# Pool totals the softmax's sums over the partitions, in place of TensorE's products with ones

## The chip, the core and the metric

The kernel runs on one core of a Trainium2 chip. A core has TensorE (matrix products, PE in the profile), VectorE (DVE), ScalarE (ACT) and GpSimd (POOL, called Pool here), each with its own queue that is worked off in order, and SyncE (SP), whose queue issues the DMAs. The metric is the device time of one execution in microseconds (us); a run's value is the median of its executions.

## The reference

A block of attention and then a small step behind it, for 4 batches of 1024 tokens with 1024 channels, all in 32-bit floats. `x` is normalized, scaled and shifted by a condition, projected to queries, keys and values of 16 heads, and each head's softmax weighs its values; the result is projected and added:

```python
xn = _rms_norm(x, g_norm) * (1.0 + scale) + shift
qkv = xn @ W_qkv                        # 16 heads of 64
q, k = _rms_norm(q, g_q), _rms_norm(k, g_k)
logits = einsum('bhqd,bhkd->bhqk', q, k) * d ** (-0.5)
attn = softmax(logits, axis=-1)
o = einsum('bhqk,bhkd->bhqd', attn, v)
x = x + o + o @ W_out
x = x + (causal convolution of x over 4 tokens, channel by channel) + b
```

## The kernel before, in words

**Units.** Two heads form a pair; a pair's 1024 queries are worked in two halves of 512. One pair and one half is a `Unit`: 4 batches x 8 pairs x 2 halves = 64 units. Keys lie on the partitions, 128 at a time (8 steps, `kt`), queries of both heads along the rows (2 x 512). For one unit:

- `scores(kts)`: TensorE writes 128 keys x 2 x 512 queries into a PSUM tile of tag "s" (two such buffers); ScalarE copies it to an `sp` tile (line 696); from the second tile on, `running` (line 705, VectorE) keeps the running maximum `mx`.
- `softmax()` calls nothing at once but puts steps on a list, each with a due time: `maximum` (line 710, one all-reduce over partitions with max on Pool), `broadcast` (line 719, ScalarE copies the result into a PSUM tile of tag "s"), and for each of the 8 tiles `shift` (line 724, VectorE subtracts) and `weigh` (line 728 on ScalarE takes the exponential; line 730 on Pool adds the tile to `sum`).
- `values(kts)`: TensorE multiplies the weights by the values into `pav` (line 751).
- `finish()`: TensorE totals `sum` over the partitions by four products with a 128 x 32 tile of ones (line 766), one for each quarter of the 1024 queries, into a PSUM tile of tag "m".
- `spread` (line 784 and on): ScalarE copies the totals to SBUF; four DMAs write 256 totals each to DRAM (line 787), and one DMA reads them back as `few`, 128 partitions x 8 (line 789).
- `invert`: VectorE takes the reciprocal of `few` (line 792), a DMA writes it to DRAM (line 794), and two DMAs read it back, repeated over 64 partitions for each head, as `rec` (line 797).
- `divide`: VectorE multiplies `pav` by `rec` (line 806), and a DMA stores the result for the output product (line 810).

The last two units (batch 3, last pair) total all 512 columns in each product and invert the totals directly on VectorE (line 804), without the DMAs.

**The order.** TensorE's, VectorE's, ScalarE's and Pool's instructions run in the order in which the program emits them. A clock in the program, `clock[0]`, decides that order: `tick(us)` moves it on by an assumed duration and then runs all deferred steps that are due, in the order of their due times; `defer(delay, key, step)` puts a step on the list, due `delay` after the clock; `need(key)` runs the steps of that key at once. A score of one tile and the values of one tile tick 0.9 each (`PAIR`), a piece of the QKV product 2.65 (`TIME`), four transposes 0.45.

The main loop goes through the 64 units. Work of other kinds (pieces of the QKV product of pairs to come, transposes, output products, stores) is cut into four stretches. For unit p, with `last` the unit before it:

```python
unit.scores((0, 1)); need("exp", last.name); last.values(range(0, HT))
fill(); unit.scores((2, 3)); fill(); last.values(range(4, 6))
unit.scores((4, 5)); last.values(range(6, NT)); last.finish()
fill(); unit.scores((6, 7)); need("mx", unit.name); unit.softmax()
defer(DIVIDE, ..., last.divide); fill()
```

The fourth `fill` is the long one (26 on the clock, 22 in batch 0); the first three are mostly empty. The due times of the softmax are counted from `softmax()`: the maximum at 2.6, the broadcast at 6.5, the subtraction of tile kt at 7.6 + kt x 1.8 (1.6 in batch 0), the exponential and the addition 1.3 after it.

**Buffers.** The tag "xs" has two buffers of 128 x 512 for squares of `x` (`Norm.squares`), for a few rows at the start and for the modulation; the tag "xg" has two of 128 x 1024, for chunks of `x` that are transposed (`Chunk.load`). `sum` and the maximum share one buffer (tag "sum").

Of the kernel before, what the change touches and what calls it, by code (L numbers as in the profile page):

```python
# [10 lines left out]
F32 = mybir.dt.float32  # L11
# [4 lines left out]
P = 128  # L16
# [5 lines left out]
def kernel(  # L22
# [32 lines left out]
    nc = tc.nc  # L55
    B, N, DIM = x.shape
    D = DIM // HEADS
    NJ = DIM // P
    NT = N // P
    HN = N // 2  # L60
# [7 lines left out]
    QN = N // 4  # L68
# [6 lines left out]
    apool = ctx.enter_context(tc.tile_pool(name="apool", bufs=1))  # L75
    small = ctx.enter_context(tc.tile_pool(name="small", bufs=2))
    ps_s = ctx.enter_context(tc.tile_pool(name="ps_s", bufs=2, space=bass.MemoryType.PSUM))
    ps_m = ctx.enter_context(tc.tile_pool(name="ps_m", bufs=3, space=bass.MemoryType.PSUM))
    dram = ctx.enter_context(tc.tile_pool(name="dram", bufs=1, space=bass.MemoryType.DRAM))
# [16 lines left out]
    def defer(delay, key, step):  # L96
        pending.append((clock[0] + delay, next(serial), key, step))
# [10 lines left out]
    def tick(us):  # L108

        clock[0] += us  # L110
        flush(lambda e: e[0] <= clock[0])
# [11 lines left out]
    def fill_gap(us):  # L123
        for e in sorted(idle, key=lambda e: e[2][2][0] != "qk"):
            if e[2] not in pending:
                idle.remove(e)
            elif e[0] <= clock[0] and e[1] <= us:
                us -= e[1]
                idle.remove(e)
                pending.remove(e[2])  # L130
                e[2][3]()
# [8 lines left out]
    def need(*key):  # L140
        flush(lambda e: e[2] == key)
# [26 lines left out]
    R_COND, R_G, R_CB, R_BE = 0, TAPS * NJ, (TAPS + 1) * NJ, (TAPS + 2) * NJ  # L168
    R_GQ = R_BE + 2 * NJ
    NR = R_GQ + 2  # L170
    rows = apool.tile([P, HN], F32, tag="xs", name="rows", bufs=2)[:NR, :P]
    nc.sync.dma_start(rows[R_COND:R_G, :], cond.rearrange("k (j p) -> (k j) p", p=P))
    nc.sync.dma_start(rows[R_G:R_CB, :], g_norm.rearrange("(j p) -> j p", p=P))
    nc.sync.dma_start(rows[R_CB:R_BE, :], conv_b.rearrange("(j p) -> j p", p=P))
# [36 lines left out]
    class Norm:  # L211


        def __init__(self, b, tiles):
            self.b, self.tiles = b, tiles
            n = len(tiles)
            self.name = f"{b}_{tiles[0]}"
            self.ss = small.tile([P, NT * 2], F32, tag="ss", name=f"ss_{self.name}", bufs=1)
            self.ss = self.ss[:, : n * 2].rearrange("p (i g) -> p i g", i=n)
            self.rn = small.tile([P, NT], F32, tag="rn", name=f"rn_{self.name}")[:, :n]  # L220

        def squares(self, i):
            t0 = self.tiles[i] * P
            for g in range(2):
                xs = apool.tile([P, HN], F32, tag="xs", name=f"xs_{self.name}_{i}_{g}", bufs=2)
                nc.sync.dma_start(xs, x[self.b, t0 : t0 + P, g * HN : (g + 1) * HN])
                defer(5.0 + g, ("x", self.name), lambda xs=xs, g=g: self.square(xs, xs, i, g))

# [2 lines left out]

        def squares_of(self, i, halves):
            for g in range(2):
                to = apool.tile([P, HN], F32, tag="xs", name=f"xs_{self.name}_{i}_{g}", bufs=2)
                self.square(halves[g], to, i, g)

        def root(self):
# [143 lines left out]
    class Embed:  # L381
# [22 lines left out]
        def run(self):  # L404
            half = self.half
            ps = ps_m.tile([P, 512], F32, tag="m", name=f"mod_ps_{half}")[:, :QN]
            for k in range(NJ):
                for g in range(4):
                    nc.tensor.matmul(
                        ps[32 * g : 32 * (g + 1), :],  # L410
                        condT[:, k, :],
                        self.w[k][g // 2][:, g % 2 * QN : (g % 2 + 1) * QN],
                        start=(k == 0),
                        stop=(k == NJ - 1),
                    )
            sb = apool.tile([P, HN], F32, tag="xs", name=f"mod_sb_{half}", bufs=2)[:, :QN]
            nc.scalar.copy(sb, ps)

            mt = ps_m.tile([P, 512], F32, tag="m", name=f"modT_ps_{half}")[:, :QN]
            mt = mt.rearrange("p (i g b) -> p i g b", i=2, g=4)  # L420
            for i in range(2):
                nc.tensor.transpose(mt[:, i].rearrange("p g b -> p (g b)"), sb[:, i * P : (i + 1) * P], ident)
            for s in range(2):
                c = s * NJ + half * KH
                nc.vector.tensor_add(
                    mod[:, c : c + KH, :].rearrange("p (u i) b -> p u i b", u=2),
                    mt[:, :, 2 * s : 2 * s + 2, :B].rearrange("p i u b -> p u i b"),
                    cols[:, R_BE + c : R_BE + c + KH]
                    .rearrange("p (u i) -> p u i", u=2)
                    .unsqueeze(3)  # L430
                    .to_broadcast([P, 2, 2, B]),
                )
            js = slice(half * KH, (half + 1) * KH)
            nc.vector.scalar_tensor_tensor(
                gain[:, js, :],
                mod[:, js, :],
                1.0,
                cols[:, R_G + half * KH : R_G + (half + 1) * KH].unsqueeze(2).to_broadcast([P, KH, B]),
                ALU.add,
                ALU.mult,  # L440
            )
# [235 lines left out]
    class Unit:  # L677
        def __init__(self, pr, half):
            self.pr, self.half = pr, half
            self.name = f"{pr.b}_{pr.c}_{half}"  # L680
            self.sp = []

# [43 lines left out]
        def weigh(self, kt):  # L726
            sp = self.sp[kt]
            nc.scalar.activation(sp, sp, AF.Exp)  # L728
            if kt:
                nc.gpsimd.tensor_tensor(self.sum, self.sum if kt > 1 else self.sp[0], sp, ALU.add)  # L730

        def softmax(self):

            key = ("exp", self.name)
            loud[0] = clock[0] + TO_SHIFT + TO_EXP
            step = STEP if self.pr.b else STEP_FIRST
            loud[1] = loud[0] + NT * step + LOUD
            defer(TO_MAX, key, self.maximum)
            defer(TO_MAX + 0.1, key, lambda: fill_gap(GAP))
            defer(TO_SPREAD, key, self.broadcast)  # L740
            for kt in range(NT):
                at = TO_SHIFT + kt * step
                defer(at, key, lambda kt=kt: self.shift(kt))
                defer(at + TO_EXP, key, lambda kt=kt: self.weigh(kt))

        def values(self, kts):
            if kts[0] == 0:
# [10 lines left out]
                tick(PAIR)  # L758

        def finish(self):  # L760
            b, c = self.pr.b, self.pr.c
            tot = ps_m.tile([P, HN], F32, tag="m", name=f"tot_{self.name}")
            for g in range(4):
                h, i = divmod(g, 2)
                some = slice(0, HN) if (b, c) == (B - 1, NJ - 1) else slice(i * QN, (i + 1) * QN)
                nc.tensor.matmul(  # L766
                    tot[32 * g : 32 * (g + 1), : some.stop - some.start],
                    ones,
                    self.sum[:, h, some],
                    start=True,  # L770
                    stop=True,
                )
            tick(2 * PAIR)
            self.tot = tot
            if (b, c) == (B - 1, NJ - 1):
                return
            key = ("tot", self.name)
            defer(0.2, key, lambda: self.spread(tot))
            defer(8.0, key, self.invert)

        def spread(self, tot):

            sums = apool.tile([P, HN], F32, tag="rec", name=f"tots_{self.name}", bufs=1)
            nc.scalar.copy(sums[:, :QN], tot[:, :QN])
            scr = dram.tile([4, QN], F32, tag=f"tot_{self.name}", name=f"scrT_{self.name}")
            for g in range(4):
                nc.sync.dma_start(scr[g : g + 1, :], sums[32 * g : 32 * g + 1, :QN])
            self.few = small.tile([P, 2 * HN // P], F32, tag="few", name=f"few_{self.name}", bufs=1)
            nc.sync.dma_start(self.few, scr.rearrange("g (p i) -> (g p) i", p=32))

        def invert(self):
            nc.vector.reciprocal(self.few, self.few)
# [6 lines left out]
        def divide(self):  # L799
            b, c = self.pr.b, self.pr.c  # L800
            need("tot", self.name)
            if (b, c) == (B - 1, NJ - 1):
                self.rec = apool.tile([P, HN], F32, tag="rec", name=f"rec_{self.name}", bufs=1)
                nc.vector.reciprocal(self.rec, self.tot)
            oT = apool.tile([P, HN], F32, tag="oT", name=f"oT_{self.name}", bufs=2)
            nc.vector.tensor_mul(oT, self.pav, self.rec)
            if (b, c) == (B - 1, NJ - 1):
                oTs[b, c, self.half] = oT
                return
            nc.sync.dma_start(scrO[b][self.half][:, c, :], oT)  # L810
# [260 lines left out]
    TO_MAX, TO_SPREAD, TO_SHIFT, TO_EXP, STEP = 2.6, 6.5, 7.6, 1.3, 1.8  # L1071
# [241 lines left out]
    for T in range(NPR):  # L1313
        for step in START.get(T, ()):
            step()
        run(piece(T))
# [6 lines left out]
    for p in range(B * NB):  # L1323
# [10 lines left out]
        def fill():  # L1334
            run(next(stretches))
# [68 lines left out]
```

## Time and profile before

| | |
|---|---|
| time, median of 3 runs | 2848.15 us (2846.98 to 2849.5) |
| span of the profiled execution, first to last instruction | 2846.5 us |
| TensorE busy / its share | 2764.2 us / 97% |
| VectorE | 2161.3 us / 76% |
| ScalarE | 1541.5 us / 54% |
| Pool | 1345.1 us / 47% |
| DMA | 509.40 MB, mean 179 GB/s |
| granted TensorE clock, mean | 0.995 |

The span leaves out what lies ahead of the first and behind the last instruction: 1.65 us by the median. A line of the profile that gives a group of instructions reads: line, engine, operation, output <- inputs, shape, count | busy us, mean ns of one | idle time of the engine just ahead of them, and what ended it. A line of a timeline reads: start us, duration us, engine, line, operation, and in brackets the idle time ahead of it and what ended it. PEld is TensorE's loading of weights, SPq the queue of SP; "x8" behind a product with four calls counts two passes of each.

### The profile page before, as it was taken

Reading aid. Unit: us, or ns where it says so; the run is one execution under the profiler, and the core shown is the slowest. Engines: PE = TensorE matmul, PEld = TensorE weight load, DVE = VectorE, ACT = ScalarE, POOL = GpSimd, SP = SyncE. Lnnn points to the kernel's source line nnn. Section 1 sums busy time; section 2 is a strip of 40 time slices with the busy share of each in tenths; the row PEclk is TensorE's granted clock in tenths of the full one; section 3 lists DMA queues with packets and bytes.
Section 4 is the critical chain, followed back from the end, with each engine's and each line's share of the span. In section 5 each row is a group of like instructions: output and inputs, shape, how many; then the busy total and the mean of one; then the engine's idle time right before and its main releaser. Section 6 shows DMA issues by size and latency. Waiting matters only on the chain.

```text
span 2846.5 us, 31973 instructions
## 1 busy us (share of the span) xinstructions
PE 2764.2 (97%) x10581; PEld 1310.7 (46%) x10581; DVE 2161.3 (76%) x2579; ACT 1541.5 (54%) x2221; POOL 1345.1 (47%) x534
## 2 busy tenths in 40 slices
PE   6999999999999999999999999999999999999998
PEld 3544444444444444444444445445444444443344
DVE  4688887888888777777877777787877877687863
ACT  4255656655555556655555556665555545555532
POOL 2056554565654453553555355355445445554520
PEclk9999999999999999999999999999999999999999
DMA  9844555644565566665565556666556444533334
GB/s 318 280 168 145 193 174 184 211 152 169 174 196 159 174 196 205 214 229 164 162 207 186 165 178 212 203 218 198 163 202 211 141 130 159 167 109 96 118 108 118
DMA packets 416844, 509.40 MB, mean 179 GB/s; under 512 B 40816, under 2 KB 326824, under 8 KB 406952
## 3 DMA queue, kind: packets, MB, share of 16 engines
q1 hardware_dynamic: 416680, 507.36, 55.1%
q8 instruction: 85, 1.39, 0.2%
q14 instruction: 79, 0.65, 0.1%
HBM read 411.85 MB, written 95.40 MB: 178 GB/s over the span
## 4 chain that ended last, share of the span: by engine, by line
PE 78%; DVE 11%; DMA 4%; ACT 3%; issue 2%; POOL 2%; SPq 1%; DVEq 0%; ACTq 0%; POOLq 0%
PE pqkv_P L648 29%; PE pav L751 15%; PE s L688 15%; PE po L1009 5%; PE po_P L940 4%; PE po L940 4%; DVE sp L724 3%; DVE mx L705 3%; POOL sum L730 1%; PE qkt L506 1%; PE tot L766 1%; DMA scrR<-few 1%; DVE qk L498 1%; PE po L995 1%; ACT sp L696 1%
## 5 line engine op out<-in xcount | busy, mean ns | idle before, releaser
L648 PE MATMUL pqkv_P<-w_P,a 128*128 128x384 f32 x3456 | 1172.5, 490 | 15.5 <-issue 5.6
L730 POOL TENSOR_TENSOR sum<-sum,sp 128x1024 f32<-128x1024 f32 x384 | 956.8, 2492 | 36.5 <-ACT sp L728 5.7
L648 PEld LDWEIGHTS pqkv_P<-w_P,a 128*128 128x128 f32 x3456 | 639.4, 190 | 478.7 <-issue 69.2
L696 ACT COPY sp<-s 128x1024 f32<-128x1024 f32 x512 | 506.0, 1015 | 507.4 <-PE s L688 459.1
L705 DVE TENSOR_TENSOR mx<-mx,sp 128x1024 f32<-128x1024 f32 x384 | 518.9, 1351 | 170.9 <-ACT sp L696 143.8
L728 ACT ACTIVATE sp<-sp 128x1024 f32<-128x1024 f32 x512 | 531.8, 1055 | 204.6 <-DVE sp L724 201.3
L724 DVE TENSOR_TENSOR sp<-sp,mbp 128x1024 f32<-128x1024 f32 x512 | 604.2, 1210 | 19.3 <-ACT mbp L719 19.3
L710 POOL PARTITION_ALL_REDUCE mb<-mx x64 | 219.2, 3426 | 826.5 <-DVE mx L705 785.0
L688 PE MATMUL s<-qT,kT 64*128 64x512 f32 x2048 | 516.3, 620 | 21.8 <-DVE sp L724 17.0
L751 PE MATMUL pav<-sp,v 128*64 128x512 f32 x2048 | 486.5, 607 | 0.0
L730 POOL TENSOR_TENSOR sum<-sp,sp 128x1024 f32<-128x1024 f32 x64 | 151.5, 2367 | 485.6 <-ACT sp L728 232.9
L688 PEld LDWEIGHTS s<-qT,kT 64*128 64x128 f32 x2048 | 174.9, 186 | 314.8 <-issue 200.0
L751 PEld LDWEIGHTS pav<-sp,v 128*64 128x64 f32 x2048 | 131.2, 137 | 331.9 <-issue 322.2
L1045 DVE SCALAR_TENSOR_TENSOR y<-x,cols,y 128x512 f32<-128x512 f32 x192 | 224.3, 1173 | 47.9 <-ACT y L1033 43.3
L705 DVE TENSOR_TENSOR mx<-sp,sp 128x1024 f32<-128x1024 f32 x64 | 113.2, 1769 | 102.1 <-ACT sp L696 102.0
L667 DVE TENSOR_TENSOR qk<-u,pqkv_P 128x256 f32<-128x256 f32 x256 | 106.2, 415 | 77.9 <-PE pqkv_P L648 76.5
L1009 PE MATMUL po<-ob,wo 128*128 128x512 f32 x352 | 155.3, 593 | 0.0
L940 PE MATMUL po_P<-o_P,wq_P 128*128 128x512 f32 x320 | 143.9, 592 | 0.0
L498 DVE TENSOR_TENSOR qk<-qk,ms 128x1024 f32<-128x1024 f32 x64 | 129.7, 2047 | 0.0
L719 ACT COPY mbp<-mb 128x1024 f32<-128x1024 f32 x64 | 65.2, 1018 | 111.0 <-POOL mb L710 111.0
L940 PE MATMUL po<-o_P,wq_P 128*128 128x512 f32 x240 | 108.0, 592 | 0.0
L485 ACT ACTIVATE sq<-qk 128x512 f32<-128x512 f32 x128 | 76.7, 627 | 53.6 <-DVE qk L667 53.6
(94 smaller groups left out, 1730.7 us busy)
## 6 DMA issues: line engine op xcount, KB each, us to landing
a<-scrA SPq DMA_DIRECT2D x212, 512.0 KB
w_P<-scrB SPq DMA_DIRECT2D x64, 768.0 KB
o_P<-scrS SPq DMA_DIRECT2D x40, 1024.0 KB
w_P<-in_L_cond_W_qkv_dram SPq DMA_DIRECT2D x192, 192.0 KB
o_P<-scrO SPq DMA_DIRECT2D x30, 1024.0 KB
scrA<-r SPq DMA_DIRECT2D x28, 896.0 KB
wq_P<-scrW SPq DMA_DIRECT2D x70, 256.0 KB
xc<-in_x_dram SPq DMA_DIRECT2D x64, 256.0 KB
```

What stands on the lines that cost most here:

```text
L648: nc.tensor.matmul(pm, (chunk.r(place) if a is None else a[:, k, :])[:, t % 2 * P : (t % 2 + 1) * P], w[:, k, :], start=(k == 0), stop=(k ...
L688: nc.tensor.matmul(ps[:, h, :], pr.kT[kt // HT][h * D : (h + 1) * D, kt % HT * P : (kt % HT + 1) * P], pr.qT[self.half][h * D : (h + 1) * ...
L696: nc.scalar.copy(sp, ps)
L705: nc.vector.tensor_max(self.mx, self.mx if kt > 1 else self.sp[0], self.sp[kt])
L710: nc.gpsimd.partition_all_reduce(self.mb.rearrange("p h q -> p (h q)"), self.mx.rearrange("p h q -> p (h q)"), P, bass_isa.ReduceOp.max,)
L724: nc.vector.tensor_sub(self.sp[kt], self.sp[kt], self.mb)
L728: nc.scalar.activation(sp, sp, AF.Exp)
L730: nc.gpsimd.tensor_tensor(self.sum, self.sum if kt > 1 else self.sp[0], sp, ALU.add)
L751: nc.tensor.matmul(self.pav[h * D : (h + 1) * D, :], self.pr.v[kt // HT][:, kt % HT, h * D : (h + 1) * D], self.sp[kt][:, h, :], start=(kt ...
L940: nc.tensor.matmul(pm, self.w[name][:, k, :], self.o[name][:, k, :], start=(k == 0 and name not in ("P2", "P3", "P4")), stop=(k == KH - 1),)
L1009: nc.tensor.matmul(self.pm, self.w[kh][:, k % KH, :], oTs[b, k, half], start=False, stop=(k == NJ - 1),)
L1045: nc.vector.scalar_tensor_tensor(self.y, self.x1[:, k : k + HN], cols[:, r : r + 1], self.y, ALU.mult, ALU.add)
```

## The change

The totals over the partitions are taken by Pool: a second all-reduce over partitions (`total`), with addition, emitted right behind the unit's last addition, in place of the four products in `finish`, for 62 of the 64 units. The last two units (`ends`) keep the products. `spread` then needs no copy by ScalarE: one DMA writes the 1024 totals from one partition to DRAM and one reads them back as 128 x 8. `spread` is due 0.2 and `invert` 9.5 after `total` (before: 0.2 and 8.0 after `finish`), and `finish` no longer ticks 1.8 for those 62 units. The new tile `tot` (128 x 1024) takes the place of the tag "xs" in SBUF; what used "xs" now uses the two buffers of "xg".

```diff
@@ class Norm, and the same in three other places
-                xs = apool.tile([P, HN], F32, tag="xs", name=f"xs_{self.name}_{i}_{g}", bufs=2)
+                xs = apool.tile([P, HN], F32, tag="xg", name=f"xs_{self.name}_{i}_{g}", bufs=2)
...
@@ class Unit
             self.pr, self.half = pr, half
+            self.ends = (pr.b, pr.c) == (B - 1, NJ - 1)
...
+        def total(self):
+
+            self.tot = apool.tile([P, 2, HN], F32, tag="tot", name=f"tot_{self.name}", bufs=1)
+            nc.gpsimd.partition_all_reduce(
+                self.tot.rearrange("p h q -> p (h q)"),
+                self.sum.rearrange("p h q -> p (h q)"),
+                P,
+                bass_isa.ReduceOp.add,
+            )
+            key = ("tot", self.name)
+            defer(0.2, key, self.spread)
+            defer(9.5, key, self.invert)
+
         def softmax(self):
...
                 defer(at, key, lambda kt=kt: self.shift(kt))
                 defer(at + TO_EXP, key, lambda kt=kt: self.weigh(kt))
+            if not self.ends:
+                defer(at + TO_EXP, key, self.total)
...
         def finish(self):
-            b, c = self.pr.b, self.pr.c
-            tot = ps_m.tile([P, HN], F32, tag="m", name=f"tot_{self.name}")
+            if not self.ends:
+                return
+            self.tot = ps_m.tile([P, HN], F32, tag="m", name=f"tot_{self.name}")
             for g in range(4):
-                h, i = divmod(g, 2)
-                some = slice(0, HN) if (b, c) == (B - 1, NJ - 1) else slice(i * QN, (i + 1) * QN)
                 nc.tensor.matmul(
-                    tot[32 * g : 32 * (g + 1), : some.stop - some.start],
+                    self.tot[32 * g : 32 * (g + 1), :],
                     ones,
-                    self.sum[:, h, some],
+                    self.sum[:, g // 2, :],
                     start=True,
                     stop=True,
                 )
             tick(2 * PAIR)
-            self.tot = tot
-            if (b, c) == (B - 1, NJ - 1):
-                return
-            key = ("tot", self.name)
-            defer(0.2, key, lambda: self.spread(tot))
-            defer(8.0, key, self.invert)
-
-        def spread(self, tot):
-
-            sums = apool.tile([P, HN], F32, tag="rec", name=f"tots_{self.name}", bufs=1)
-            nc.scalar.copy(sums[:, :QN], tot[:, :QN])
-            scr = dram.tile([4, QN], F32, tag=f"tot_{self.name}", name=f"scrT_{self.name}")
-            for g in range(4):
-                nc.sync.dma_start(scr[g : g + 1, :], sums[32 * g : 32 * g + 1, :QN])
+
+        def spread(self):
+
             self.few = small.tile([P, 2 * HN // P], F32, tag="few", name=f"few_{self.name}", bufs=1)
-            nc.sync.dma_start(self.few, scr.rearrange("g (p i) -> (g p) i", p=32))
+            scr = dram.tile([1, 2 * HN], F32, tag=f"tot_{self.name}", name=f"scrT_{self.name}")
+            nc.sync.dma_start(scr, self.tot[0:1, :, :].rearrange("o h q -> o (h q)"))
+            nc.sync.dma_start(self.few, scr.rearrange("o (p i) -> (o p) i", p=P))
```

More of the change, by code (lines that the diff above doesn't have):

```diff
@@ L170 @@
     NR = R_GQ + 2
-    rows = apool.tile([P, HN], F32, tag="xs", name="rows", bufs=2)[:NR, :P]
+    rows = apool.tile([P, HN], F32, tag="xg", name="rows", bufs=2)[:NR, :P]
     nc.sync.dma_start(rows[R_COND:R_G, :], cond.rearrange("k (j p) -> (k j) p", p=P))
@@ L233, in squares_of @@
             for g in range(2):
-                to = apool.tile([P, HN], F32, tag="xs", name=f"xs_{self.name}_{i}_{g}", bufs=2)
+                to = apool.tile([P, HN], F32, tag="xg", name=f"xs_{self.name}_{i}_{g}", bufs=2)
                 self.square(halves[g], to, i, g)
@@ L415, in run @@
                     )
-            sb = apool.tile([P, HN], F32, tag="xs", name=f"mod_sb_{half}", bufs=2)[:, :QN]
+            sb = apool.tile([P, HN], F32, tag="xg", name=f"mod_sb_{half}", bufs=2)[:, :QN]
             nc.scalar.copy(sb, ps)
@@ L801, in divide @@
             need("tot", self.name)
-            if (b, c) == (B - 1, NJ - 1):
+            if self.ends:
                 self.rec = apool.tile([P, HN], F32, tag="rec", name=f"rec_{self.name}", bufs=1)
@@ L806, in divide @@
             nc.vector.tensor_mul(oT, self.pav, self.rec)
-            if (b, c) == (B - 1, NJ - 1):
+            if self.ends:
                 oTs[b, c, self.half] = oT
```

## The prediction

> **What bounds the kernel now.** I read the page first: shares by engine and the chain that ended last.
>
> ```profile
> PE 2764.2 (97%) x10581; PEld 1310.7 (46%) x10581; DVE 2161.3 (76%) x2579; ACT 1541.5 (54%) x2221; POOL 1345.1 (47%) x534
> ...
> PE 78%; DVE 11%; DMA 4%; ACT 3%; issue 2%; POOL 2%; SPq 1%; DVEq 0%; ACTq 0%; POOLq 0%
> ```
>
> TensorE is busy 97% and carries 78% of the chain; VectorE carries 11%, so there are places where TensorE waits for it. Pool is busy 47% and nearly absent from the chain. Next the groups with shapes kept apart, and the chain from 1300 to 1400 us: the price of what goes and of the nearest thing to what comes.
>
> ```profile
> L766 PE MATMUL tot<-sum,ones 128*32 128x256 f32 x496 | 39.6, 391 | 3.4 <-POOL sum L730 3.4
> L710 POOL PARTITION_ALL_REDUCE mb<-mx x64 | 219.2, 3426 | 826.5 <-DVE mx L705 785.0 <-DVE u L663 28.4 <-PE otp L1056 13.1
> ...
> 1368.64 0.57 PE tot L766 x8
> ```
>
> The products with ones overlap one another (four products, eight passes): they hold TensorE's chain for 0.57 us a unit. An all-reduce of the same 128x1024 shape takes Pool 3.4 us.
>
> Then the timelines of Pool, TensorE, VectorE and SP (start, duration, what; idle time before in brackets). Pool, for a unit of batch 0 and two of batch 1:
>
> ```profile
> 251.62 3.25 POOL L710 PARTITION_ALL_REDUCE mb<-mx  x1 [6.99 <-DVE mx L705]
> 265.24 16.43 POOL L730 TENSOR_TENSOR sum<-sum,sp 128x1024 f32<-128x1024 f32 x6 [0.46 <-ACT sp L728]
> 289.22 3.33 POOL L710 PARTITION_ALL_REDUCE mb<-mx  x1 [7.55 <-DVE mx L705]
> ...
> 1335.64 3.25 POOL L710 PARTITION_ALL_REDUCE mb<-mx  x1 [15.09 <-DVE mx L705]
> 1349.46 15.44 POOL L730 TENSOR_TENSOR sum<-sum,sp 128x1024 f32<-128x1024 f32 x6
> 1374.21 3.25 POOL L710 PARTITION_ALL_REDUCE mb<-mx  x1 [9.31 <-DVE mx L705]
> ...
> 1387.19 14.91 POOL L730 TENSOR_TENSOR sum<-sum,sp 128x1024 f32<-128x1024 f32 x6 [0.45 <-ACT sp L728]
> ```
>
> The additions end late: at 281.67, 1364.90 and 1402.10, where the next unit's first score on TensorE starts at 268.95, 1355.5 and 1397.9. I call that first score A; the additions end at A+12.7, A+9.4 and A+4.2. Idle time before the next maximum is 7 to 15 us, so 3.4 us more of Pool fits.
>
> ```profile
> 268.95 1.13 PE L688 MATMUL s<-qT,kT 64*128 64x512 f32 x4
> 271.37 1.13 PE L688 MATMUL s<-qT,kT 64*128 64x512 f32 x4 [1.29 <-DVE sp L724]
> ...
> 278.24 7.17 DVE L705 TENSOR_TENSOR mx<-mx,sp 128x1024 f32<-128x1024 f32 x4 [1.00 <-ACT sp L696]
> 286.43 2.56 DVE L705 TENSOR_TENSOR mx<-mx,sp 128x1024 f32<-128x1024 f32 x2 [1.02 <-ACT sp L696]
> ...
> 294.99 0.20 DVE L792 RECIPROCAL few<-few 128x8 f32<-128x8 f32 x1
> ```
>
> The second score waits for VectorE's last subtraction of the unit before (it frees the PSUM buffer of the broadcast maximum). So in batch 0 a late maximum is a late TensorE, one to one. And the reciprocal L792 now stands behind all seven running maxima L705, and waits for nothing.
>
> ```profile
> 1371.69 1.12 SPq L787 DMA_DIRECT2D scrT<-tots  x4
> ...
> 1625.66 0.34 SPq L789 DMA_DIRECT2D few<-scrT  x1
> ...
> 1629.82 0.20 DVE L792 RECIPROCAL few<-few 128x8 f32<-128x8 f32 x1 [1.54 <-DMA few<-scrT]
> ...
> 2623.50 0.35 SPq L789 DMA_DIRECT2D few<-scrT  x1
> ...
> 2625.08 0.20 DVE L792 RECIPROCAL few<-few 128x8 f32<-128x8 f32 x1 [1.34 <-DMA few<-scrT]
> ```
>
> Where the reciprocal did wait for its transfer, that took 4.2 us and 1.6 us from issue.
>
> **What goes.** 62 of 64 units lose four products: 62 x 0.57 = 35 us of TensorE; the last two units keep theirs. ScalarE loses 62 copies of 0.38 us and SP 186 issues of about 0.3 us, all beside other work: SP waited for that copy in every unit, 763 us in all (waits of SP's queue). Whatever else binds, 35 us is all that TensorE can win, plus the 3.4 us it waited for sums.
>
> **The all-reduce itself.** 62 x 3.4 = 212 us on Pool, hidden in its idle time as shown; without that cover it would be 3.4 us a unit. The trace has it with max only; an addition is taken at the same 3.4 us, with bounds 2.4 (Pool's own addition of this shape, 2.49 us, rounded down) and 6.8 (twice). The Trainium skill, "GPSIMD Engine Reference", Performance versus the Vector engine, gives 247,699 ns for a reduction along partitions at 128x2048, which speaks against the change: half of that is an estimate of 124 us a unit, over 7 ms in all. The row shows 3.4 us for this instruction, and ScalarE's copy of its result starts 3.28 us after its start (1335.64 to 1338.92), so I go by the row.
>
> **The reciprocal moves, and this is what costs.** `invert` is due 9.5 on the planner's clock after `total`, and `total` is called with the last exponential, no longer after the next unit's values. From the code: after A the clock takes 0.9 for each score and value in the order s0 s1 v0-v3 s2 s3 v4 v5 s4 s5 v6 v7 s6 s7, and each maximum is due 1.2 after its score begins: mx2 at A+6.6, mx3 7.5, mx4 10.2, mx5 11.1. Batch 0: the stretch behind softmax (call its start S) is 7 products of 2.65 and two transposes of 0.45, so A = S+19.45; the last exponential is due at S+7.6+7x1.6+1.3 = S+20.1, runs at the next tick, A+0.9, and `invert` is due at A+10.4: behind mx4, ahead of mx5 to mx7. Later batches (step 1.8): long stretches (about S+27, 27 units) run the last exponential at A-3.1, `invert` at A+6.4, ahead of mx2 to mx7; short ones (about S+23, 18 units) run it at A, `invert` at A+9.5, ahead of mx4 to mx7. VectorE works in order, so these maxima, then the unit's maximum on Pool, its broadcast, its subtractions and every PSUM eviction of the QKV products behind them wait for the reciprocal; it waits for Pool's total and two trips through DRAM.
>
> Trips: the four writes begin at 1333.12 and the read is issued at 1335.18, so one write takes 1.2 to 2; the read 1.6 to 4.2; with 0.1 for the hand-over 2.9 to 6.3. I take 3.5, near the low end, because SP issues nothing else in that stage (none from 1358.8 to 1371.69).
>
> That closes a ring from unit to unit: maximum, shifts, additions, total, trips, reciprocal, remaining maxima, next maximum. Its length: batch 0, from 251.62 to 281.67 = 30.05, + 3.4 + 3.5 + 0.2 + 3 maxima of 1.28 + 0.2 = 41.2 us. The mean distance of Pool's maxima there is (750.88 - 177.08)/15 = 38.25 us. 17 units x 2.9 = +49 us. Long units: 1374.21 to 1402.10 = 27.9, + 7.1 + 6 x 1.28 + 0.2 = 42.9; short: 1335.64 to 1364.90 = 29.3, + 7.1 + 5.1 + 0.2 = 41.7; weighted 42.4 against (2669.93 - 787.87)/45 = 41.8: 45 x 0.6 = +27 us. Seven of these distances are already 44.3 to 46.0 us (1031.02 to 1076.53 is one; more output work lies there): the ring is not the limit in them, and what they exceed it by, 17 us together, can't be saved up for the others, so it is added back: +17. Sum: 49 + 27 + 17 = +93 us. The 35 us are not subtracted, since TensorE now stands waiting at the second score.
>
> **Moved at no cost.** `spread` goes ahead on SP's queue, to about A, where it holds SP until the total ends: 1364.9 + 3.4 = 1368.3, where SP now stands until 1371.69. Loads queued behind are due two product pairs later, after the 15.6 us of scores and values; if that cover fails, some us a unit, mostly hidden by the ring. The tag "xs" merged into "xg": the squares of a batch run one double ahead of its chunks, so the two buffers are free; otherwise 48 loads of 256 KB would wait, 1.5 us each at the page's 179 GB/s. `finish` without its tick of 1.8 moves deferred steps a product later at most.
>
> **Rivals.** *TensorE's saving shows (faster).* If the transfers are back before VectorE reaches the reciprocal, or the delay fits into the slack ahead of the second score, only the products go: 2848 - 35 = 2813. It decides at total plus trips under about 3 us a unit, or additions ending by A+3. For it: in long units the last subtraction ends 5 to 6 us before A. Against: batch 0 has no such slack (1.29 us wait above). *The addition is slow.* At 6.8 us instead of 3.4 every ring is 3.4 longer: 62 x 3.4 = +211 on top, about 3152. Against: the loop moves the same data as for max. *The ring half hidden.* Additions end earlier once VectorE works undisturbed, ring 1 us shorter: 93 - 62 = +31, 2879. *No effect*: 35 us gained and as much lost, a coincidence.
>
> **How the numbers follow.** The span is 2846.5 us and the median of the runs 2848.15, so 1.65 us lies around the span; 2848 + 93 = 2941. Chances: the ring as summed 0.68, half hidden 0.12, slow addition 0.08, TensorE's saving 0.09, no effect 0.03. A measurement tells about 0.2% (5.7 us) from no change. Range: trips of 2.9 give -0.6 x 62 = -37, and the half hidden ring reaches down to 2879; trips of 5 give +1.5 x 62 = +93, 3034. So 2879 to 3034; a slow addition and TensorE's saving, 0.17 together, are left out.
>
> **What would show it.** Right: L766 with 16 products left; 62 all-reduces of about 3.4 us into tot right behind the additions; the reciprocal of few idle for 3 to 7 us before it, released by its transfer, with maxima behind it; TensorE idle before scores, released by VectorE's subtractions; Pool's maxima some 41 us apart in batch 0. Wrong: a reciprocal that never waits, or TensorE still solid with a period 0.57 us shorter, or TensorE waiting for transfers of weights instead.

## The result, and the profile after

The changed kernel takes 3461.95 us (median of 4 runs, 3459.31 to 3464.06) beside 2848.43 us for the kernel before on the same chip: 1.2153 times as long, interval 1.2136 to 1.217. The forecast was slower, at 2941 us; the true loss is 613 us, nearly seven times the 93 forecast.

The page of the changed kernel, first the busy shares, then the chain that ended last:

```profile
PE 2888.5 (84%) x10085; PEld 1369.0 (40%) x10085; DVE 2166.4 (63%) x2579; ACT 1527.5 (44%) x2159; POOL 1720.5 (50%) x596
...
POOL 33%; DVE 20%; PE 17%; issue 16%; DMA 8%; ACT 4%; SPq 1%; POOLq 0%; DVEq 0%; ACTq 0%
```

TensorE carried 78% of the chain before and carries 17% now. Pool carries 33%, although it is busy only half the span, and "issue", time in which an engine waited for nothing that the profile shows, has grown from 2% of the chain to 16%. The groups with shapes kept apart say where:

```profile
L736 POOL PARTITION_ALL_REDUCE tot<-sum x62 | 380.5, 6137 | 372.5 <-issue 372.5
L711 POOL PARTITION_ALL_REDUCE mb<-mx x64 | 216.3, 3380 | 688.8 <-DVE mx L706 688.8
L798 DVE RECIPROCAL few<-few 128x8 f32<-128x8 f32 x62 | 12.6, 203 | 681.9 <-DMA few<-scrT 681.9
L781 PE MATMUL tot<-sum,ones 128*32 128x512 f32 x16 | 3.0, 833 | 3.5 <-POOL sum L731 3.5
```

The total takes 6.14 us, where the maximum over the same shape takes 3.38; and ahead of each total Pool stands 372.5 / 62 = 6.0 us for no visible reason. VectorE stands 11 us in the mean before each of the 62 reciprocals, until the transfer lands. Of the products with ones 16 are left.

One unit of batch 0, from maximum to maximum, in the timelines of Pool, then SP and VectorE (start, duration, what; idle time before it in brackets):

```profile
287.83 3.23 POOL L711 PARTITION_ALL_REDUCE mb<-mx  x1 [6.93 <-DVE mx L706]
...
301.38 16.43 POOL L731 TENSOR_TENSOR sum<-sum,sp 128x1024 f32<-128x1024 f32 x6 [0.47 <-ACT sp L729]
323.75 6.13 POOL L736 PARTITION_ALL_REDUCE tot<-sum  x1 [5.94 <-issue]
336.90 3.38 POOL L711 PARTITION_ALL_REDUCE mb<-mx  x1 [7.02 <-DVE mx L706]
```

```profile
329.91 0.24 SPq L794 DMA_DIRECT2D scrT<-tot  x1
331.12 0.33 SPq L795 DMA_DIRECT2D few<-scrT  x1
```

```profile
314.38 5.84 DVE L706 TENSOR_TENSOR mx<-mx,sp 128x1024 f32<-128x1024 f32 x3 [1.01 <-ACT sp L697]
332.76 0.20 DVE L798 RECIPROCAL few<-few 128x8 f32<-128x8 f32 x1 [12.54 <-DMA few<-scrT]
332.88 3.85 DVE L706 TENSOR_TENSOR mx<-mx,sp 128x1024 f32<-128x1024 f32 x3
```

Here the ring of the prediction can be read off whole. The additions end at 301.38 + 16.43 = 317.81, 29.98 after the maximum began. Then 5.94 of "issue", 6.13 of total, 2.88 to the reciprocal at 332.76, 0.12, three maxima of together 3.85, and 0.17 to the next maximum: 49.07 us. No other wait is in it. All over, Pool's maxima are 49.24 us apart in batch 0 (38.25 before) and 51.17 in the later batches (41.82 before). Counted as in the prediction, 17 x 10.99 + 45 x 9.35 = 608 of the 613 us.

### The profile page after: what moved, and what is told of

Its sections match the earlier page's. It is cut to its first block, busy times and chain, and to the rows that moved or that the text cites. A ratio compares the mean times of both kernels' runs of the same rounds, so it can differ in the third digit from the quotient of the medians.

```text
span 3457.2 us, 30756 instructions
## 1 busy us (share of the span) xinstructions
PE 2888.5 (84%) x10085; PEld 1369.0 (40%) x10085; DVE 2166.4 (63%) x2579; ACT 1527.5 (44%) x2159; POOL 1720.5 (50%) x596
## 4 chain that ended last, share of the span: by engine, by line
POOL 33%; DVE 20%; PE 17%; issue 16%; DMA 8%; ACT 4%; SPq 1%; POOLq 0%; DVEq 0%; ACTq 0%
POOL sum L731 21%; POOL tot L736 10%; DVE mx L706 8%; PE pqkv_P L648 8%; DVE sp L725 4%; PE po L1015 4%; DMA few<-scrT 3%; ACT sp L729 2%; DMA scrT<-tot 2%; PE po_P L946 2%; DVE qk L498 2%; PE s L689 1%; POOL mb L711 1%; PE pav L767 1%; DVE qk L667 1%
## 5 line engine op out<-in xcount | busy, mean ns | idle before, releaser
L648 PE MATMUL pqkv_P<-w_P,a 128*128 128x384 f32 x3456 | 1276.7, 523 | 269.6 <-DVE v L667 107.7
L648 PEld LDWEIGHTS pqkv_P<-w_P,a 128*128 128x128 f32 x3456 | 685.2, 204 | 791.9 <-issue 285.1
L736 POOL PARTITION_ALL_REDUCE tot<-sum x62 | 380.5, 6137 | 372.5 <-issue 372.5
L706 DVE TENSOR_TENSOR mx<-mx,sp 128x1024 f32<-128x1024 f32 x384 | 521.0, 1357 | 70.1 <-ACT sp L697 39.8
L798 DVE RECIPROCAL few<-few 128x8 f32<-128x8 f32 x62 | 12.6, 203 | 681.9 <-DMA few<-scrT 681.9
L1051 DVE SCALAR_TENSOR_TENSOR y<-x,cols,y 128x512 f32<-128x512 f32 x192 | 236.7, 1237 | 49.6 <-ACT y L1039 45.0
L506 PE MATMUL qkt<-ident,qk 128*128 128x128 f32 x512 | 85.2, 294 | 95.2 <-DVE v L667 62.8
L946 PE MATMUL po_P<-o_P,wq_P 128*128 128x512 f32 x320 | 152.8, 623 | 11.7 <-DVE u L663 6.5
```

What stands on the lines that cost most here:

```text
L648: nc.tensor.matmul(pm, (chunk.r(place) if a is None else a[:, k, :])[:, t % 2 * P : (t % 2 + 1) * P], w[:, k, :], start=(k == 0), stop=(k ...
L706: nc.vector.tensor_max(self.mx, self.mx if kt > 1 else self.sp[0], self.sp[kt])
L736: nc.gpsimd.partition_all_reduce(self.tot.rearrange("p h q -> p (h q)"), self.sum.rearrange("p h q -> p (h q)"), P, bass_isa.ReduceOp.add,)
L946: nc.tensor.matmul(pm, self.w[name][:, k, :], self.o[name][:, k, :], start=(k == 0 and name not in ("P2", "P3", "P4")), stop=(k == KH - 1),)
L1051: nc.vector.scalar_tensor_tensor(self.y, self.x1[:, k : k + HN], cols[:, r : r + 1], self.y, ALU.mult, ALU.add)
```

## The experiments

**Pool by itself** (`micro`). A list of instructions for Pool alone, with nothing of the reference computed, to see what the "issue" is. Its calls, written out from their loops:

```
tt(s); reduce(red["addTT"], s, "add")           # reads what the addition wrote
tt(s); reduce(red["addTTfree"], free, "add")    # reads something else
tt(s); reduce(red["maxTT"], s, "max")
...
reduce(red["add4"], free, "add")                # four in a row; max the same
reduce(red["maxafter"], free, "max"); reduce(red["addafter"], free, "add")
...
nc.gpsimd.memset(s, 1.0); reduce(red["addms"], free, "add")
```

> This kernel computes nothing of the reference: Pool alone works off a list of additions (tensor-tensor, 128x1024), all-reduces with add and with max, each after an addition whose result it reads, after an addition that it has nothing to do with, several in a row, at 512 and 256 columns, and behind a wait for VectorE. Theory 'switch': going from additions to all-reduces costs Pool some 5.9 us of idle time before the all-reduce, and about 6.7 us back, whichever operation it is and whether or not it reads the addition's result; between all-reduces in a row, add or max in any order, there is none; behind a wait that lasts longer than 6 us (VectorE) it does not show. Rival 'drain': the idle time is the wait for the addition's result to land; then it is gone where the all-reduce reads another tile. Rival 'add is another library': the idle time stands also between max and add in a row. Size: add 6.1 us and max 3.3 us at 1024 columns; if the cost goes by columns, 3.1 and 1.6 at 512.

Pool's timeline in it:

```profile
41.84 6.13 POOL L40 PARTITION_ALL_REDUCE addTT<-s  x1 [5.82 <-issue]
55.09 2.33 POOL L37 TENSOR_TENSOR s<-s,b 128x1024 f32<-128x1024 f32 x1 [7.12 <-issue]
...
105.46 6.13 POOL L40 PARTITION_ALL_REDUCE addTTfree<-free  x1 [5.70 <-issue]
...
191.09 3.24 POOL L40 PARTITION_ALL_REDUCE maxTT<-s  x1 [6.07 <-issue]
...
322.65 24.82 POOL L40 PARTITION_ALL_REDUCE add<-free  x4
347.38 13.25 POOL L40 PARTITION_ALL_REDUCE max<-free  x4
360.54 3.30 POOL L40 PARTITION_ALL_REDUCE maxafter<-free  x1
363.74 6.19 POOL L40 PARTITION_ALL_REDUCE addafter<-free  x1
...
451.86 6.13 POOL L40 PARTITION_ALL_REDUCE addwait<-late  x1 [13.31 <-DVE late L65]
...
594.00 1.03 POOL L68 MEMSET s<- 128x1024 f32 x1
594.94 6.21 POOL L40 PARTITION_ALL_REDUCE addms<-free  x1
```

Between an addition of two tensors and an all-reduce Pool stands 5.5 to 6.1 us, whether or not the all-reduce reads what the addition wrote, and for max as for add; on the way back 6.6 to 7.7. Between all-reduces, of either kind, nothing lies, nor between a memset and an all-reduce. So it is neither the addition draining nor a library of the add of its own: it is a switch between two kinds of Pool work. The Trainium skill, "GPSIMD Engine Reference", 2.1 Instruction dispatch, states an IRAM load of about 6 us, without a visible profile instruction, for the first call to a freshly loaded kernel; the rows agree in size, and show a cost at every change of kind, not at the first alone; that it is such a load is not shown by any run. One all-reduce itself takes 6.13 (add) and 3.24 (max).

Where VectorE is late anyway, the switch doesn't show: the all-reduces that wait 13 us for a VectorE result start right behind it (0.14 us in the row at 451.86). That fits the kernel before, where each maximum waited longer than the switch takes and the profile put the whole wait down to VectorE.

**The max in the add's place** (`as_max`), so that Pool's total is shorter and all else stays.

```
-                bass_isa.ReduceOp.add,
+                bass_isa.ReduceOp.max,
```

> The changed kernel with max in place of add in the total (so the totals are maxima and the output is not the reference's); the order is unchanged. Theory 'ring': each unit's ring is shorter by 6.13 - 3.38 = 2.75 us, 62 units: 3462 - 170 = about 3290 us (3275 to 3310). The 5.9 us of idle time ahead of the total stay. Rival 'the total's length is hidden': within 10 us of 3462. As predicted blind (3.4 us and no idle time ahead of it) it would be 2941.

The total's row:

```profile
L736 POOL PARTITION_ALL_REDUCE tot<-sum x62 | 202.0, 3259 | 366.5 <-issue 366.5
```

3277.55 us, ratio 1.1512 (1.1495 to 1.1529): 184 us less than the changed kernel, 3.0 a unit, where the total is 6137 - 3259 = 2878 ns shorter. The "issue" ahead of it stays, 5.9 us a unit. A microsecond of Pool's total is a microsecond of the period, as the ring has it.

**The reciprocal behind all maxima** (`late`). This opens the ring on VectorE and leaves Pool as it is.

```
         def total(self):
...
-            defer(9.5, key, self.invert)
...
         def finish(self):
             if not self.ends:
+                defer(9.8, ("tot", self.name), self.invert)
                 return
```

> The changed kernel with one step moved: the reciprocal is again due after the next unit's values (9.8 after finish), behind all running maxima, where it stood before. Pool's total and the two transfers stay. Theory 'ring through VectorE' (maxima wait behind the reciprocal): the ring is cut there; what is left is Pool's own chain, maximum to last addition (30.0 us in batch 0, 27.9 or 29.3 later) + switch 5.9 + total 6.1 + 0.2 = 42.2, 40.1 or 41.5 us, against 38.25 and 41.8 before: about +4 x 17 = +67 in batch 0, and -0.57 or nothing a unit later: 2870 to 2920 us. Rival 'Pool's occupancy': the 12 us more on Pool are what costs, wherever the reciprocal stands: 3400 or more. Rival 'SP held by the early transfer': no change either, 3400 or more, since spread stays where it is.

3065.58 us, ratio 1.0766 (1.0749 to 1.0783). The largest part of the loss goes, 396 us of 613, so the ring through the reciprocal was real; but about 218 us stay that this theory had no place for. Where they lie, a stretch of batch 1 shows, VectorE first, then Pool:

```profile
1451.58 12.02 DVE L706 TENSOR_TENSOR mx<-mx,sp 128x1024 f32<-128x1024 f32 x6
```

```profile
1453.54 6.58 POOL L736 PARTITION_ALL_REDUCE tot<-sum  x1 [5.99 <-issue]
1463.77 3.23 POOL L711 PARTITION_ALL_REDUCE mb<-mx  x1 [3.65 <-DVE mx L706]
```

Six maxima that take 7.83 us in a unit of batch 1 of the changed kernel, where Pool stands still beside them, take 12.02 here without a gap, and Pool's total lies inside. Just one of the six is held: the third takes 5.37 us and ends half a microsecond ahead of the total; the others take 1.23. Over the whole kernel the 76 maxima that lie for the most part beside a total take 3.68 us in the mean, median 4.92, beside 1.23 where Pool is idle; 47 of the 62 totals hold one of these maxima each, for 5.2 us in the mean, and the other 15 hold none. VectorE's subtractions, whose second input is in PSUM, keep 1.21 us beside Pool's additions; beside a total none of them lies here. In the changed kernel this hardly shows (mean 1357 ns there), since VectorE stands at the reciprocal during the total.

**The total beside the products** (`unread`). The products with ones, their copy and their transfers stay as before; Pool makes its total too, and nobody reads it.

```
-            defer(0.2, key, self.spread)
-            defer(9.5, key, self.invert)
...   (finish, spread and invert as before the change)
```

> The kernel before, products with ones, copy and transfers as they were, and beside them Pool's total into a tile that nothing reads. Theory 'ring through VectorE': no ring by the reciprocal; Pool's own chain is 42.2 us in batch 0 against 38.25 (+67) and 40.1 or 41.5 later against 41.8 (0 to +20): 2900 to 2940 us. Rival 'Pool's occupancy': 3400 or more.

3038.62 us, ratio 1.0673 (1.0655 to 1.0691), above the 2900 to 2940 expected. Nobody waits for this total, and it costs 191 us: the same kind of loss as in `late`, so that loss comes from the instruction's presence on Pool, not from the way its result takes. (The merged tag "xg" stays in this kernel; in `late_from1` below, which has it too, batch 0 without Pool's totals keeps its period, 38.2 us.) I then had two causes for it: Pool's own queue grown too long (switch 5.9 and total 6.1 ahead of the next maximum), and VectorE's maxima held while the total runs. Four kernels were to tell them apart.

**The max in `late`** (`late_max`) **and the totals from batch 1 on** (`late_from1`).

```
-                bass_isa.ReduceOp.add,        # late_max
+                bass_isa.ReduceOp.max,
...
+            self.pe = pr.b < FROM             # late_from1, FROM = 1: these units total with products, as before
-            if not self.ends:
+            if not self.ends and not self.pe:
                 defer(at + TO_EXP, key, self.total)
```

> As `late`, with max instead of add in Pool's total (3.25 us instead of 6.13; the output is then not the reference's). Theory 'held' (VectorE's maxima stand still for as long as the all-reduce runs, and the maximum on Pool waits for them in every unit): 62 x 2.9 = -180, 2886, within 2870 to 2920. Rival 'chain' (only batch 0 is limited by Pool's queue): 17 x 2.9 = -49, 3016. Rival 'neither' (the planner's changed order costs it): 3065.

> As `late`, but only from batch 1 on (45 units); batch 0 totals with products on TensorE as in the kernel before. In `late` the distance of Pool's maxima in batch 0 was 43.65 us against 38.25 before, so batch 0 should give back 17 x 5.4 = 92. Theory 'held': the later batches keep their loss, 44.5 against 41.8: 2848 + 45 x 2.7 = 2970, within 2940 to 2990. Rival 'chain' (only batch 0 has too little room on Pool): 2848 - 45 x 0.57 = 2822.

`late_max` took 2901.56 us (ratio 1.0175, 1.0158 to 1.0192), 164 less than `late`: 2.6 us in each of 62 units, near the 180 of 'held' and far from the 49 of 'chain'. `late_from1` took 2983.58 (1.047, 1.0454 to 1.0487), within what 'held' gave: Pool's maxima are 38.16 us apart in batch 0, as before, and 44.56 in the later batches, where Pool's queue alone has room: between total and maximum Pool stands 2.3 us in the median there, for VectorE's maxima. (The profile has 46 totals by Pool; the expectation counted 45.) `late_max` by itself doesn't tell a held VectorE from a Pool queue that binds in every unit, since the shorter total shortens both; the next pair was to tell.

**Maxima that read PSUM** (`late_ps`, and its control `before_ps`). TensorE's scores are read where they were written, so that VectorE has one input in SBUF instead of two.

```
-                    defer(1.2, ("mx", self.name), lambda kt=kt: self.running(kt))
+                    defer(1.2, ("mx", self.name), lambda kt=kt, ps=ps: self.running(kt, ps))
...
-            nc.vector.tensor_max(self.mx, self.mx if kt > 1 else self.sp[0], self.sp[kt])
+            nc.vector.tensor_max(self.mx, self.mx if kt > 1 else self.sp[0], ps)
```

> As the kernel `late` (reciprocal behind all maxima), but the running maxima read the scores from PSUM, where TensorE wrote them, instead of ScalarE's copy in SBUF; everything else stays. Theory 'held': in `late` VectorE's operations with two inputs in SBUF stand still while Pool's all-reduce runs (running maxima of 1.2 us became 4.9), and this delays the next maximum in all 62 units. With one input in PSUM they should keep 1.2 us beside the all-reduce; what stays is batch 0, where Pool's own chain is too long: from maximum to the end of the additions 30.05 us, switch 5.9, total 6.1, so 42.2 against 38.25, 17 x 4 = 68. So 2848 + 68 - 26 (45 units x 0.57 of TensorE) = 2890, within 2860 to 2930, and at most 70 us above the kernel `before_ps`. Rival 'chain' (Pool's queue alone, VectorE's standing still is hidden): no better than `late`, 3040 to 3090. Rival 'PSUM held longer' (each score tile is now freed by VectorE's maximum, 2 buffers): both this kernel and `before_ps` lose alike.

> The kernel before, with the running maxima reading the scores from PSUM; the control for `late_ps`. In the kernel before they take 2.7 us where they overlap Pool's additions and 1.23 us alone; read from PSUM they should take 1.2 to 1.3 us throughout, so the maximum on Pool comes some us earlier. Against that, a score's PSUM buffer is freed by VectorE instead of ScalarE, so the third score onward waits for the maximum of the one two before. Theory: same or a little faster, 2810 to 2850. Rival: the buffers bind and it is slower, 2880 to 2960.

The group of the maxima in `late`, then in `late_ps`:

```profile
L706 DVE TENSOR_TENSOR mx<-mx,sp 128x1024 f32<-128x1024 f32 x384 | 709.5, 1848 | 100.8 <-ACT sp L697 68.3 <-DVE mx L706 1.8 <-ACT ot L1066 0.5
```

```profile
L706 DVE TENSOR_TENSOR mx<-mx,s 128x1024 f32<-128x1024 f32 x384 | 468.8, 1221 | 292.7 <-ACT sp L697 272.4 <-DVE mx L706 1.4
```

With one input in PSUM they keep 1.22 us; the 139 of them that lie beside a total take 1221 ns in the mean. So being held goes with the second SBUF input. The Trainium skill, "SBUF — State Buffer", Who interferes with whom, states it so: a VectorE instruction with two SBUF inputs contends with a GpSimd instruction that reads SBUF, and the loser blocks for the whole instruction. The rows of `late` agree: the held maximum of 5.37 us lasts until just before the end of the total beside it.

The times: `late_ps` 3003.91 us (1.0537, 1.0521 to 1.0553), `before_ps` 2928.09 (1.0272, 1.0257 to 1.0288). I had hoped for a control that costs nothing; it costs 78 us, since a score's PSUM buffer is now freed by VectorE (TensorE's loads for the scores wait 175 us for the maxima in it). So `late_ps` missed its 2890, but it stands 76 us above its control, where 70 was the bound, and `late` stands 218 above its own. If the two costs add, VectorE held makes up some 140 of the 218, and what is left is Pool's longer queue, most of it in batch 0 (41.39 us between maxima beside 38.23 in the control: 17 x 3.2 = 54). That split is an estimate: in the later batches the control's period is itself longer (43.4 us instead of 41.8), which gives Pool more room, so part of the 140 may be Pool's.

**The total directly behind the next maximum** (`behind_from1`, `behind`, then two more). If the switch is what costs, two all-reduces in a row need none between them. The total of a unit is put right behind the next unit's maximum, from batch 1 on, or in all units. In lines left out below, the maximum's result moves to the buffer of `tot` and the total to that of the running maximum `mx`, the reciprocal is due 12 behind the total, and the division at 20.

```
             defer(TO_MAX, key, self.maximum)
+            if last is not None and not last.ends and not last.pe:
+                defer(TO_MAX, key, last.total)
...
-            if not self.ends and not self.pe:
-                defer(at + TO_EXP, key, self.total)
```

> From batch 1 on (45 units) Pool's total of a unit stands directly behind the next unit's maximum, so that two all-reduces follow each other and no switch lies between them; batch 0 totals on TensorE as before. The reciprocal is due 12 behind the maximum, among the subtractions, which read PSUM, and the division at 20 instead of 18. Theory (the loss of the changed kernel is made of Pool's switch, the total ahead of the next maximum, and VectorE's operations on SBUF held beside it): Pool has 3.25 + 6.1 + switch 6.7 + additions 17.3 + switch 5.9 = 39.3 us of work a unit in a period of 41.8, so TensorE's saving shows: 2848 - 45 x 0.57 = 2822, 2810 to 2845. Rival 'held at another place': the products q and k by their norms and the combinations of weights, which VectorE does between maximum and first subtraction, are held for the 6.1 us, the subtractions come 4 us late and only the long units hide it: 2848 + 18 x 4 - 26 = 2894. Rival 'all-reduce in itself' (it costs where it stands): 2980 or more.

> The same in all 62 units. In batch 0 the period is 38.25 us and Pool's work 39.3, so 17 x 1 = 17 us are lost there against 35 won by TensorE: 2848 + 17 - 35 = 2830, 2815 to 2860. Rival 'held at another place' as for the other kernel: 2900 or more, and batch 0 then loses most.

Both are slower, far above their theory: 3167.03 us (1.1113, 1.109 to 1.1136) and 3303.59 (1.1597, 1.1575 to 1.162). The total's idle time ahead is gone (4.6 us in all in `behind_from1`), but VectorE's gap work (the products q and k by their norms, the combinations) lies beside it, and the division waits for the reciprocal's second trip. From VectorE's timeline and waits in `behind_from1`:

```profile
1527.58 7.07 DVE L922 TENSOR_TENSOR S<-S 128x512 f32<-128x512 f32 x4
```

```profile
DVE oT L834 <- DMA rec<-scrR: 299.6, 49, 9.6
```

The four combinations of sums take 2.86 us in the kernel before. The next two kernels were to take these two costs away: `behind_direct_from1` has ScalarE make the reciprocal from Pool's total on all partitions, with no DMA; `behind_clear_from1` also issues the gap work behind the last subtraction.

```
+                nc.scalar.activation(self.rec[r, :], self.tot[r, h, :], AF.Ln)    # for each head
+            nc.scalar.activation(self.rec, self.rec, AF.Exp, scale=-1.0)
...
-            defer(TO_MAX + 0.1, key, lambda: fill_gap(GAP))        # this and the next line: behind_clear_from1 alone
+            defer(TO_MAX + 0.1 if last is None or last.ends or last.pe else at_last + 0.05, key, lambda: fill_gap(GAP))
```

> As `behind_from1`, but without the trips through DRAM: Pool's total is already on all partitions, and ScalarE makes the reciprocal from it by Ln and Exp, due 9 behind the maximum; the division is due at 18 again. In `behind_from1` VectorE's division waited for the reciprocal's transfer 300 us in all, 49 times (about 6 us a unit, behind loads on SP's queue), and its work between maximum and first subtraction was held by the all-reduce. This kernel takes away the first only: 3167 - 45 x 4 = 2985, within 2930 to 3050. If the wait for the transfer was hidden: 3130 or more. If the held work was hidden: 2830 or less.

> As `behind_direct_from1`, and VectorE's gap work (norms of q and k, combinations of weights and sums) is issued behind the last subtraction instead of right behind the maximum, so that nothing with two inputs in SBUF stands beside Pool's total. If held VectorE work and the transfers are all that the all-reduce costs besides Pool's own time, this comes to TensorE's saving: 2848 - 26 = 2822, within 2810 to 2870. If Pool's queue is itself too long (39.3 us of 41.8 by my count), it stays above 2900.

3056.01 us (1.0745, 1.0718 to 1.0771) and 3129.09 (1.0995, 1.0971 to 1.1019), both above their ranges. Without the trips it is 111 us faster; moving the gap work made it 73 worse instead of better. The expectation's other branch was Pool's queue. One unit in Pool's timeline of `behind_clear_from1`:

```profile
1516.22 3.25 POOL L714 PARTITION_ALL_REDUCE mb<-mx  x1 [18.30 <-DVE mx L709]
1519.57 6.12 POOL L739 PARTITION_ALL_REDUCE tot<-sum  x1
1536.07 2.33 POOL L734 TENSOR_TENSOR sum<-sp,sp 128x1024 f32<-128x1024 f32 x1 [10.38 <-ACT x L1056]
1538.48 17.38 POOL L734 TENSOR_TENSOR sum<-sum,sp 128x1024 f32<-128x1024 f32 x6
1562.40 3.25 POOL L714 PARTITION_ALL_REDUCE mb<-mx  x1 [6.54 <-DVE mx L709]
```

46.2 us from maximum to maximum, against 39.3 by my count, and hardly any slack in them: 6.54 us before the last maximum, where the switch takes some 5.9. The way back to the additions took 10.4 us instead of 6.7, though the exponentials that the first addition needs were ready; and since the additions now reach into the next unit's maxima, the two slow each other (the additions 2.66 us in the mean, 2.47 before; the maxima 1.66, 1.41 before).

Pool's queue is not the limit throughout, though. The maximum at 1516.22 came after 18.30 us of waiting for VectorE; over 43 units of the later batches Pool stood 10.0 us in the median between additions and maximum, and in only 14 of them less than 6.6. The chain that ended last agrees:

```profile
PE 47%; DVE 33%; ACT 5%; POOL 5%; issue 4%; DMA 4%; SPq 1%; DVEq 0%; ACTq 0%; POOLq 0%
```

So why this kernel loses is not settled: in some units Pool has hardly any slack, in more of them it waits for VectorE's maxima. Nor do these four kernels put out the rival 'all-reduce in itself' (2980 or more), which all four times fit. No version here beats the kernel before.

## Why the prediction was wrong in size

- **The ring: right.** Pool's total delays the reciprocal, the reciprocal the maxima behind it on VectorE, these the next maximum. The reciprocals wait as foretold, with three maxima behind them in most units of batch 0, six in 26 of the later units and four in 14 (foretold: 27 and 18), and taking the reciprocal out of the order gives back 396 us.
- **The failed step: "The all-reduce itself"**, in both of its halves. *Its duration* was taken from the maximum's row at 3.4 us; the add takes 6.14. That lay within the bounds given (2.4 to 6.8), but the value and the range went by the lower end, and the slow addition got a chance of 0.08. The reason given against it, that the loop moves the same data as for max, doesn't carry: at the same shape `micro` has 6.13 us for add and 3.24 for max. *Its cover*: "Idle time before the next maximum is 7 to 15 us, so 3.4 us more of Pool fits." That idle time is not free: some 6 us of it are the switch between additions and all-reduce. The page called it "DVE mx", since VectorE's maxima came later still. The sign was there: of the 63 maxima that follow on additions none started less than 5.99 us after the end of the additions, and no additions less than 6.67 us after the end of a maximum. Moving an all-reduce right behind the additions lays the switch bare, and the sum put it at nothing: 6.0 us in each of 62 units.
- **What it makes of the sum.** Each ring gets 5.9 + 2.7 - 0.6 (most trips took 2.9, not 3.5) = 8.0 us more: 49.2, 50.9 and 49.7 instead of 41.2, 42.9 and 41.7. The 17 us that the sum added back for seven long units fall away, since no distance before (at most 46.0 us) is longer than these rings. So 49 + 27 + 62 x 8.0 = 572, or 3420 us, of the 3462 measured. The other 42 us lie mostly in the later units with six maxima behind the reciprocal: 52.6 us instead of 50.9 in each of 26. Their additions end 0.5 us later than in the unit that the sum took, the trips take 3.35 us in the mean, and the maxima 0.5 us more. Batch 0 (49.24) and the units with four maxima (49.2) come out within half a microsecond.
- **The rivals.** TensorE's saving doesn't show: TensorE is idle 16% of the span. The slow addition came true in its price (6.1 us) and fell short for want of the switch. The half hidden ring is out.
- **Moved at no cost: nothing of it shows.** In the waits the only transfer that VectorE waits for every unit is the reciprocal's; the longest wait of TensorE's products is for VectorE (108 us).
- **Not thought of:** VectorE held beside the total. In the changed kernel it is hidden by the reciprocal's wait; it appears once that wait is gone, and with Pool's longer queue makes a loss of 218 us in `late`, and of 191 in `unread`, where nobody waits for the total.

## What to carry to other kernels

Before an instruction is moved into an engine's idle time, ask what that idle time would be if its named releaser came at once: the least idle time over all units, not the mean, shows a fixed cost hidden under a wait. On Pool, changing between tensor additions and all-reduces is such a cost, 6 to 7 us each way, and it is paid per change, not per instruction. And work given to an engine with time to spare also takes from its neighbour: here a Pool instruction of 6 us held one of VectorE's maxima with two SBUF inputs in 47 of 62 units, while maxima with one input in PSUM kept their 1.22 us.

## What the runs showed of the hardware

- An all-reduce over 128 partitions costs by the columns and by the operation: at 1024 columns 6.13 us for add and 3.24 for max, at 512 about 3.3 and 1.9, at 256 about 1.9 and 1.15 (runs of three in a row in `micro`). The 247,699 ns weighed in the prediction, which the Trainium skill, "GPSIMD Engine Reference", 3.2 Cross-partition, gives for `tensor_reduce`, are not what this instruction takes.
- The way from all-reduce back to additions took 6.6 to 7.7 us in `micro`, and up to 12.1 in `behind_clear_from1`. There it tended to be longer where the DMA engines were busier (by the load of the DMA engines in that time, the lowest third of the units has a mean of 7.5 us, the other two 9.3 and 9.1); no run tested whether that is the cause.
- The granted clock of TensorE was lower in the kernels in which TensorE was busy for less of the span: 0.995 in the kernel before (97%), 0.986 in `before_ps` (96%), 0.969 in `late` (92%), 0.912 in the changed kernel (84%), where a QKV product takes 523 ns instead of 490. With TensorE on 17% of the chain I read this as an effect more than a cause of the loss; that was not tested by itself.
